# Gathered groups of a graph layer: plain row fetches, sums by quarters and a one-hot placement

## The chip, the cores and the metric

The kernel runs on one core of one Trainium2 chip. The metric is the device time of the launch in microseconds (us). The core has a matrix engine (TensorE, PE in the profile; its weight loads are PEld), a vector engine (VectorE, DVE), an activation engine (ScalarE, ACT), a general engine (GpSimd, POOL) and a queue engine that issues most transfers (SyncE, SP). Each works through its own list of instructions in order and waits for the others by semaphores.

## The reference

One layer of a graph network on 6250 nodes with 64 features and 206250 edges, sorted by the node they point to:

```
h   = relu(layernorm(x))
msg = h[src] + edge_feat
agg = segment_sum(msg, dst, 6250)
out = x + relu(agg @ W1 + b1) @ W2 + b2
```

W1 is 64 x 128 and W2 is 128 x 64. All is float32. `h[src]` is a lookup of one row per edge, and `segment_sum` adds the rows that share a destination. On average a node has 33 edges.

## The kernel before

The edges are padded to 202 **groups** of 1024 (`G`; eight per partition, `J = 8`). They are treated in two ways.

**Counted groups** (the first 178, `GA`). The nodes that they reach are cut into 22 **blocks** of 252 nodes (`NW = 22`). For a block, `count` makes a matrix that says how many edges go from each source node to each of the block's nodes. It takes 14 steps per block: in every second step DVE makes two one-hot tiles (`hot_lo` and `hot_key`, L702), in each step PE multiplies six pairs of them into PSUM (L712) and ACT copies the counts to bfloat16 (L714). One block later PE multiplies the counts with h, which is kept in three bfloat16 parts (`product`, L747 and L750). So h[src] is never fetched for these edges. Their edge features are summed apart, in chunks of 42 nodes: `load` brings a chunk (SP queue, L375), `chunk_hot` makes a one-hot of 21 columns on DVE (L384), `chunk_sum` multiplies one-hot and features in four column groups of PE, a quarter of the chunk's edges in each (L396), ACT copies the result (`by_node`, L399), and `chunk_place` puts the four quarters to their columns by a constant 0/1 matrix (`select`, L408) inside the block's PSUM.

**Gathered groups** (the last 24, `GP = 24`) reach the rest of the nodes. `load_h` brings a group's edge features (SP queue, L824, one transfer of 256 KB) into a tile `pfeat` of four buffers. `fetch_h` then issues eight indirect transfers on the POOL queue (`gather`, L256), each of which fetches one row of h per partition from a table in device memory and **adds** it to `pfeat` on the way. The groups go in pairs. `sum_groups` makes a one-hot of 42 columns for each of the two (`hotp`, L425), multiplies the summed rows with it (16 matmuls, features as the weights, two column groups, L429), ACT copies the result (`sum_p`, L432), and `add_sums` adds it to the node sums `agg` at a column that is read into a register (L418).

After that, each block goes through the two dense layers (`mlp_hidden` L799, `mlp_product` L806, `mlp_add` L813, `mlp_store` L817).

**Order of the work.** The order of instructions is written out by hand (`manual_schedule`). A loop over 310 steps calls `count` for each, and a table `before`, a list `later` and some counters put all else between the steps. Where a pair of gathered groups goes is planned: `queue` holds what POOL has still to issue, each with a planned cost (`GATHER_US = 2.12` for a row gather, `WORDS_US = 2.6` for two gathers of edge words), `clock(n)` is the planned time of step n (1.7 us per step in the first block, 1.35 us behind it), and a pair is put behind step n when the planned end of its gathers, and 4 us (`LAND_US`), lie before `clock(n)`. What has not found a place by the last step follows behind the loop. The planner only sets the order; on the chip, engines wait for what has not come yet.

**The opening** (until about 41 us) finds where each block's edges lie: gathers of `rows` and `words` on POOL, searches on ACT (`seek`, L272), the packing of source and destination into one word per edge (`dstn`, two operations of DVE, L515, which need the source numbers that PE has turned and ACT copied to `srcl`, L505), a write of the packed list (L518, issued from ACT's list), and the layer norm. L510 copies to `row2` the first node of each gathered group, spread by PE over the partitions (`pe`, L509).

The lines that the change touches, cut to the core:

```
parts_of[g] = work.tile([P, J, D], F32, name="pfeat", bufs=4)            # load_h
gather(parts_of[g][:, j, :], table, src_p[:, ...j:...j+1], OP.add)       # fetch_h
hot = work.tile([P, J, W], F32, tag="hot", name="hotp")                  # sum_groups, W = 42
nc.tensor.matmul(pa[k:k + D, b, :], tiles[b][:, j, :], hot[:, j, :], ...)  # k = 0 or 64
to = agg[:, ds(bases.pop(g + b), W)]                                     # add_sums
nc.vector.tensor_tensor(to, to, pa[:, b, :], op=OP.add)
```

Of the kernel before, what the change touches and what calls it, by code (L numbers as in the profile page):

```python
# [9 lines left out]
F32 = mybir.dt.float32  # L10
# [8 lines left out]
P = 128  # L19
N = 6250  # L20
E = 206250
D = 64
# [15 lines left out]
W = 42  # L38
# [10 lines left out]
WR = 128  # L49
WR_BITS = 7  # L50
# [4 lines left out]
GP = 24  # L55
# [16 lines left out]
NW = 22  # L72
# [26 lines left out]
GATHER_US = 2.12  # L99
WORDS_US = 2.6  # L100
# [8 lines left out]
def gnn_kernel(ctx: ExitStack, tc: tile.TileContext, x, src_t, dst_t, dst_g, edge, w1, b1, w2, b2, out):  # L109
# [34 lines left out]

    firstp_i = small.tile([1, GP], I32, name="firstp_i")
    nc.scalar.dma_start(firstp_i.rearrange("o (q h k) -> o q h k", h=2, k=1),
                        dst_g[GA // 2:G // 2, :, 0:1].unsqueeze(0))
# [44 lines left out]
    edge_w = small.tile([P, 4], F32, name="edge_w")  # L192
    for k, of in enumerate((1.0 - W, 0.5, WQ - 0.5, SPAN - 0.5)):
        nc.gpsimd.memset(edge_w[:, k:k + 1], of)
# [16 lines left out]
    select = consts.tile([P, W], F32, name="select")  # L211
    nc.gpsimd.memset(select, 1.0)
    for q in range(JQ):
        part = select[q * QP:(q + 1) * QP, :]
        nc.gpsimd.affine_select(part, part, pattern=[[1, W]], compare_op=OP.is_equal, fill=0.0, base=-QS[q],
                                channel_multiplier=-1)
        nc.gpsimd.affine_select(part, part, pattern=[[0, W]], compare_op=OP.is_ge, fill=0.0, base=WQ - 1,
                                channel_multiplier=-1)
# [36 lines left out]
    def gather(rows, source, index, op=OP.bypass):  # L255
        nc.gpsimd.indirect_dma_start(out=rows, out_offset=None, in_=source,  # L256
                                     in_offset=bass.IndirectOffsetOnAxis(ap=index, axis=0), compute_op=op)
# [24 lines left out]
    dst_p = consts.tile([P, GP, J], I32, name="dst_p")  # L282
    rel_p = dst_p.bitcast(F32)
# [74 lines left out]
    bank = ps.tile([P, GB * D], F32, name="bank", bufs=1)  # L358
# [54 lines left out]
    def add_sums():  # L413
        for g, pa in to_add:
            for b in range(GB):
                done_at[g + b] = max(made)
                to = agg[:, ds(bases.pop(g + b), W)]
                nc.vector.tensor_tensor(to, to, pa[:, b, :], op=OP.add)  # L418
        to_add.clear()

    def sum_groups(g, tiles):
        pa = bank[:, :GB * W].rearrange("p (b w) -> p b w", b=GB)
        for b in range(GB):
            hot = work.tile([P, J, W], F32, tag="hot", name="hotp")
            nc.vector.tensor_tensor(hot, rel_p[:, g - GA + b, :].unsqueeze(2).to_broadcast([P, J, W]),  # L425
                                    iota[:, :W].unsqueeze(1).to_broadcast([P, J, W]), op=OP.is_equal)
            for j in range(J):
                k = j % 2 * D
                nc.tensor.matmul(pa[k:k + D, b, :], tiles[b][:, j, :], hot[:, j, :],  # L429
                                 start=(j < 2), stop=(j >= J - 2))  # L430
        sum_p = work.tile([P, GB, W], F32, name="sum_p", bufs=1)
        nc.scalar.activation(sum_p, pa, AF.Copy)  # L432
        to_add.append((g, sum_p))
# [72 lines left out]
    firstp = small.tile([1, GP], F32, name="firstp")  # L506
    nc.vector.tensor_copy(firstp, firstp_i)
    pe = ps.tile([P, GP], F32, tag="po", name="pe", bufs=1)
    nc.tensor.matmul(pe, ones[0:1, :], firstp, start=True, stop=True)  # L509
    nc.scalar.activation(row2[:, GA:], pe, AF.Copy)  # L510
# [20 lines left out]
    pools[0].__exit__(None, None, None)  # L531
    counts.append(ctx.enter_context(pools[1]).tile([P, HI, BN + NX * V], BF16, name="counts1"))
# [13 lines left out]
    src_p = consts.tile([P, GP * J], I32, name="src_p")  # L546
    nc.sync.dma_start(src_p, src_t[:, GA * J:])
    nc.sync.dma_start(dst_p, dst_t.rearrange("p (g j) -> p g j", j=J)[:, GA:, :])

    def table_rows(index, tmp):  # L550

        nc.vector.tensor_scalar(tmp, index, LO_BITS, None, op0=OP.logical_shift_right)
        nc.vector.tensor_scalar(index, index, P - 1, None, op0=OP.bitwise_and)
        nc.vector.scalar_tensor_tensor(index, index, float(HI), tmp, op0=OP.mult, op1=OP.add)

    def find_groups():

        nc.vector.tensor_scalar(base_i[:, GA:], row2[0:1, GA:], 0.0, float(N - 1), op0=OP.max, op1=OP.min)
        nc.vector.tensor_tensor(rel_p, dst_p, row2[:, GA:].unsqueeze(2).to_broadcast([P, GP, J]), op=OP.subtract)
# [96 lines left out]
    bad = small.tile([P, 9], F32, name="bad")  # L656
    found = small.tile([1, 5], F32, name="found")

    def outside(k):
        over = late.tile([P, NWIN + NX], BF16, tag="part", name="over")[:, :GP * J]  # L660
        nc.scalar.activation(over, rel_p.rearrange("p g j -> p (g j)"), AF.Relu, scale=1.0 if k else -1.0,
                             bias=edge_w[:, 0:1] if k else 0.0, accum_out=bad[:, k:k + 1])

    def inside(n):
        which, k = divmod(n, 2)
        a = (keys[:, 1, :, 0], rel[:, :NC].rearrange("p c q k -> p (c q k)"))[which]
        over = late.tile([P, NWIN + NX], BF16, tag="part", name="over")[:, :a.shape[1]]
        nc.scalar.activation(over, a, AF.Sign, scale=-1.0 if k else 1.0,  # L668
                             bias=edge_w[:, (1, 3 - which)[k]:(2, 4 - which)[k]], accum_out=bad[:, n + 2:n + 3])

    def limits():
        nc.vector.tensor_reduce(bad[:, 6:9], bad[:, :6].rearrange("p (n k) -> p n k", k=2), AX.X, OP.add)
        nc.vector.tensor_tensor(needed, row2[0:1, GA:], needed, op=OP.is_lt)
        nc.vector.tensor_reduce(found[:, 3:4], needed, AX.X, OP.max)
        pb = ps.tile([P, 3], F32, tag="po", name="pb", bufs=1)
        nc.tensor.matmul(pb, ones, bad[:, 6:9], start=True, stop=True)
        known["b"] = pb
# [3 lines left out]
    def limits_found():  # L681
        pb = known.pop("b")
        nc.vector.tensor_scalar(found[:, 0:1], pb[:1, 0:1], 0.0, None, op0=OP.is_gt)
        nc.vector.tensor_scalar(found[:, 1:3], pb[:1, 1:3], 2.0 * EA, None, op0=OP.not_equal)
        nc.vector.tensor_reduce(found[:, 4:5], found[:, :4], AX.X, OP.add)
        nc.vector.tensor_copy(odd_i, found[:, 4:5])
# [133 lines left out]
    parts_of = {}  # L820

    def load_h(g):
        parts_of[g] = work.tile([P, J, D], F32, name="pfeat", bufs=4)
        nc.sync.dma_start(parts_of[g].rearrange("p j d -> p (j d)"),  # L824
                          edge[g * P * J:(g + 1) * P * J, :].rearrange("(p j) d -> p (j d)", j=J))
# [5 lines left out]
    def fetch_h(g):  # L831
        if g not in parts_of:
            load_h(g)
        for j in range(J):
            queue.append((GATHER_US, lambda j=j: gather(
                parts_of[g][:, j, :], table[:, :], src_p[:, (g - GA) * J + j:(g - GA) * J + j + 1], OP.add)))
        queue.append((0.0, lambda: fetched.setdefault(g, pool[0])))
# [9 lines left out]
    def features_h(g):  # L847
        read_bases(g, GB)
        sum_groups(g, [parts_of.pop(g + b) for b in range(GB)])
        for b in range(GB):  # L850
            if g + 4 + b < G:
                fetch_h(g + 4 + b)
# [10 lines left out]
    table_rows(src_p, src_hi)  # L863
# [9 lines left out]
    fetch_pair(2)  # L873
    for k in range(3):
        norm_h(k)
    load(1)
    for g in range(GA + 2, GA + 4):
        load_h(g)
    todo = {}

    def then(k, f):
# [3 lines left out]
        1: [lambda: seek(12, 3), lambda: chunk_nodes(0)],  # L885
# [3 lines left out]
        5: [lambda: place(12, 3)],  # L889
        7: [lambda: norm_b(0)],  # L890
        9: [lambda: norm_b(1)],
        11: [lambda: norm_b(2)],
        13: [find_groups],
# [12 lines left out]
        112: [lambda: outside(1)],  # L906
        116: [lambda: inside(0)],
# [77 lines left out]
    for n, (b, s) in enumerate(steps):  # L985
# [23 lines left out]
        if n >= 3:  # L1009
            if h_next < G and fetched.get(h_next + 1, 1e9) + LAND_US <= clock(n):  # L1010
                features_h(h_next)
                h_next += GB
                add_later(n + 5)
            if n == 3:
                pool[0] = clock(n - 1) + OPENING_US
            pool_until(clock(n) + LAND_US)
# [31 lines left out]
    while h_next < G:  # L1048
        features_h(h_next)
        h_next += GB  # L1050
# [14 lines left out]
    odd = nc.values_load(odd_i, min_val=0, max_val=4)  # L1065
    with tc.If(odd > 0):
# [20 lines left out]
        with tc.For_i(0, G, 1) as g:  # L1087
            feat = work.tile([P, J, D], F32, tag="pfeat", bufs=4, name="feat2")
            hsrc = work.tile([P, J, D], F32, tag="pfeat", bufs=4, name="hsrc")
# [16 lines left out]
            with tc.For_i(0, more, 1) as w:  # L1106
                hot = work.tile([P, J, WR], F32, tag="hotr", bufs=1, name="hotr")
# [51 lines left out]
```

## Time and profile before

| what | value |
| --- | --- |
| time, three runs | 511.65, 514.52 and 520.31 us, median 514.52 us |
| the profiled execution | 511.06 us, of which 509.4 us between its first and last instruction (the span) |
| granted TensorE clock | 0.991 |
| busy share of the span | PE 87%, PEld 75%, DVE 82%, ACT 71%, POOL 81% |
| instructions | 19099 |
| bytes moved | 79.04 MB in 113544 packets, 155 GB/s |

The profile is one execution. Busy times are a sum over each engine, so the same span holds all of them beside each other. "Issue" is time in which an engine waited for nothing that the profile shows. A group of instructions is told by line, engine, operation and tiles, with its count, its busy time and the mean of one. The chain of work is followed back from the last instruction, each step to what released it.

### The profile page before, as it was taken

The page shows a single profiled execution, that of the slowest core. Times are in us where ns is not written, and L with a number is a line of the kernel's source. Part 1 is how long each engine was busy: PE and PEld are TensorE (multiplying, and loading weights), DVE is VectorE, ACT ScalarE, POOL GpSimd, SP SyncE. Part 2 cuts the span into 40 slices and gives each one's busy share as a digit, 9 for nine tenths or more (in the row PEclk, how much of TensorE's full clock was granted, in tenths as well). Part 3 has the DMA queues.
Part 4 walks back from the last instruction along what each step waited for, and adds up shares of the span by engine and source line. Part 5 has one row for each costly group of instructions (what it writes and reads, how often), then busy time and mean ns, then how long its engine had stood idle before and what let it go on. Part 6 is the DMA issues. An engine that isn't in the chain of part 4 may idle for free.

```text
span 509.4 us, 19099 instructions
## 1 busy us (share of the span) xinstructions
PE 442.5 (87%) x8183; PEld 380.9 (75%) x8184; DVE 416.8 (82%) x632; ACT 359.1 (71%) x530; POOL 412.0 (81%) x265
## 2 busy tenths in 40 slices
PE   1226678889999988989989999999999999999893
PEld 1115557778888877778878888888888988888782
DVE  4789999698999969979879879799698798698521
ACT  6648867678777656997757777767777777667611
POOL 6676888888874888889888888888888888898880
PEclk9999899999999999999999999999999999999997
DMA  8848722566686566565665676586675766846560
GB/s 235 250 127 276 204 31 59 118 166 165 170 219 188 141 153 161 140 144 163 146 173 108 145 191 145 147 191 147 152 188 144 194 148 140 200 105 153 118 146 17
DMA packets 113544, 79.04 MB, mean 155 GB/s; under 512 B 32920, under 2 KB 108686, under 8 KB 113230
## 3 DMA queue, kind: packets, MB, share of 16 engines
q1 hardware_dynamic: 83962, 65.99, 43.5%
q0 software_dynamic: 29200, 10.25, 17.0%
q10 hardware_dynamic: 292, 1.52, 1.0%
q8 instruction: 66, 1.08, 0.9%
q14 instruction: 24, 0.20, 0.1%
HBM read 73.74 MB, written 3.99 MB: 153 GB/s over the span
## 4 chain that ended last, share of the span: by engine, by line
PE 69%; DVE 17%; issue 4%; ACT 4%; DMA 3%; POOL 1%; DVEq 0%; ACTq 0%; POOLq 0%
PE pc L712 21%; PE pv L747 19%; PE pv L750 11%; PE bank L396 9%; DVE hot_key L702 6%; DVE hot_lo L702 5%; PE pv L408 3%; PE ph L799 2%; PE po L806 2%; PE bank L429 2%; ACT counts L714 2%; DMA rows<-in_dst_g,row_i 1%; DMA dstq<-in_dst_g,cols_i 1%; ACT over L668 1%; POOL rows L256 1%
## 5 line engine op out<-in xcount | busy, mean ns | idle before, releaser
L256 POOL DMA_INDIRECT pfeat<-table,src_p x192 | 361.4, 1882 | 61.3 <-issue 55.2
L714 ACT ACTIVATE counts<-pc 128x882 bf16<-128x882 f32 x310 | 276.8, 908 | 48.5 <-PE pc L712 33.9
L712 PE MATMUL pc<-hot_key,hot_lo 128*128 128x147 bf16 x1860 | 174.0, 231 | 25.8 <-DVE hot_key L702 13.8
L712 PEld LDWEIGHTS <-hot_lo 128*128 128x128 bf16 x1860 | 134.2, 99 | 49.3 <-DVE hot_key L702 18.1
L702 DVE TENSOR_TENSOR hot_lo<-iota_lo,keys 128x1536 bf16<-128x1536 bf16 x155 | 147.9, 954 | 26.6 <-PE pc L712 26.0
L702 DVE TENSOR_TENSOR hot_key<-iota_key,keys 128x1776 bf16<-128x1776 bf16 x155 | 167.0, 1078 | 0.0
L747 PE MATMUL pv<-counts,h 128*128 128x252 bf16 (+1 forms) x1078 | 147.8, 271 | 0.1
L747 PEld LDWEIGHTS <-h 128*128 128x128 bf16 x1078 | 98.7, 97 | 8.0 <-issue 0.2
L750 PE MATMUL pv<-counts,h 128*64 128x252 bf16 (+1 forms) x1078 | 75.4, 274 | 0.0
L399 ACT ACTIVATE by_node<-bank 128x128 f32<-128x128 f32 x66 | 18.4, 278 | 58.2 <-PE bank L396 58.2
L396 PE MATMUL bank<-feat,hot 128*21 128x64 f32 x3168 | 58.6, 223 | 0.7 <-DVE hot L384 0.7
L396 PEld LDWEIGHTS bank<-feat,hot 128*21 128x21 f32 x3168 | 47.2, 102 | 13.7 <-issue 10.7
L750 PEld LDWEIGHTS <-h 128*64 128x64 bf16 x1078 | 53.9, 111 | 3.3 <-issue 0.2
L384 DVE TENSOR_TENSOR hot<-rel,iota 128x504 f32<-128x504 bf16 x66 | 44.8, 679 | 6.4 <-PE bank L429 5.5
L425 DVE TENSOR_TENSOR hotp<-dst_p,iota 128x336 f32<-128x336 f32 x24 | 11.7, 504 | 17.4 <-PE bank L396 17.2
L256 POOL DMA_INDIRECT words<-packed,first_i x15 | 20.5, 1367 | 4.6 <-issue 3.7
L256 POOL DMA_INDIRECT rows<-in_dst_g,row_i x15 | 17.0, 1132 | 8.7 <-ACT inrow L272 3.0
L408 PE MATMUL pv<-select,by_node 128*64 128x42 f32 x264 | 21.1, 243 | 0.0
L408 PEld LDWEIGHTS pv<-select,by_node 128*64 128x64 f32 x264 | 13.2, 136 | 8.3 <-issue 0.6
L801 ACT ACTIVATE hid<-ph,b1s 128x252 f32<-128x252 f32 (+1 forms) x25 | 11.7, 466 | 8.4 <-PE ph L799 7.2
L759 DVE TENSOR_TENSOR sums<-sums,pv 128x252 f32<-128x252 f32 x22 | 9.0, 411 | 9.6 <-PE pv L750 9.6
L799 PE MATMUL ph<-sums,w1s 128*128 128x252 f32 (+1 forms) x50 | 15.4, 390 | 1.6 <-DVE sums L418 1.1
(172 smaller groups left out, 259.0 us busy)
## 6 DMA issues: line engine op xcount, KB each, us to landing
feat<-in_edge SPq DMA_DIRECT2D x132, 384.0 KB
pfeat<-in_edge SPq DMA_DIRECT2D x24, 256.0 KB
pfeat<-table,src_p POOLq DMA_INDIRECT x192
out_y<-y SPq DMA_DIRECT2D x24, 63.0 KB
xs<-in_x SPq DMA_DIRECT2D x4, 315.0 KB
dstn<-in_dst_g SPq DMA_DIRECT2D x1, 1024.0 KB
table<-xl SPq DMA_DIRECT2D x2, 512.0 KB
packed<-dstn ACTq DMA_DIRECT2D x1, 768.0 KB
```

Source lines behind the costliest of these rows:

```text
L256: nc.gpsimd.indirect_dma_start(out=rows, out_offset=None, in_=source, in_offset=bass.IndirectOffsetOnAxis(ap=index, axis=0), compute_op=op)
L384: nc.vector.tensor_tensor(hot_of[u][:, :n].rearrange("p c j w -> p (c j) w"), rel[:, c:c + n].rearrange("p c q k -> p (c q k)").unsqueeze( ...
L396: nc.tensor.matmul(bank[q * QP:q * QP + WQ, i * D:(i + 1) * D], hot[:, i, j, :], feat[i][:, j, :], start=(k == 0), stop=(k == JP - 1))
L399: nc.scalar.activation(by_node[u][:, :n].rearrange("p c d -> p (c d)"), bank[:, :n * D], AF.Copy)
L408: nc.tensor.matmul(pvs[b][0][i * D:(i + 1) * D, a:a + CN], of[:, i, :], select, start=False, stop=False)
L425: nc.vector.tensor_tensor(hot, rel_p[:, g - GA + b, :].unsqueeze(2).to_broadcast([P, J, W]), iota[:, :W].unsqueeze(1).to_broadcast([P, J, ...
L702: nc.vector.tensor_tensor(hot.rearrange("p t (m o) -> p t m o", o=2), iota_k.rearrange("p (m o) -> p m o", o=2).unsqueeze(1).to_broadcast( ...
L712: nc.tensor.matmul(pc[:, k, m * K:(m + 1) * K], hot_lo[:, j, :], hot_key[:, j, :K], start=True, stop=True)
L714: nc.scalar.activation(counts[b % 2][:, :, s * ST * V:(s + 1) * ST * V].rearrange("p h (k m) -> p h k m", k=2), pc[:, :, :ST // 2 * K].rea ...
L747: nc.tensor.matmul(pv, h3[:, h, :2 * D], of, start=(h == 0 and not clear), stop=False)
L750: nc.tensor.matmul(pv[k:k + D, :], h3[:, h, 2 * D:], of, start=False, stop=(h >= HI - 2))
L799: nc.tensor.matmul(ph[:, :n], w1s, agg[:, start[b]:start[b + 1]], start=True, stop=True)
```

## The change

Gathered groups grow from 24 to 32, and the blocks of counts shrink from 22 to 21. With them go 6 of the 132 chunks, one of 15 lists of words and one of 5 lists of chunk destinations.

`fetch_h` fetches rows of h **without the addition**, into a tile of its own (`hsrc`, four buffers). `pfeat` keeps two buffers and the edge features alone; it is loaded by four transfers of 64 KB per group, since a group's edges now lie by quarters: quarter q of the group (256 edges in order) sits in two of the eight columns of all partitions.

The sums go as in the chunks: the one-hot has 21 columns and is made once per pair, each of a group's 16 tiles (8 of `pfeat`, 8 of `hsrc`) is a matmul with the one-hot as weights in the column group of its quarter, ACT copies the four partial results (`by_group`). Two steps later `place_groups` makes a one-hot `sel` on DVE from the quarters' offsets (`off_p`) and PE places the quarters with it into 52 columns of the same PSUM bank. `add_sums` adds from that bank, 64 partitions per group.

```
-W = 42
+W = 52
-GP = 24
+GP = 32
+PQ = 4
+PK = J // PQ
-NW = 22
+NW = 21
-GATHER_US = 2.12
-WORDS_US = 2.6
+GATHER_US = 1.4
+WORDS_US = 2.7
...
+    def hot_groups(g):
+        hot = work.tile([P, GB, J, WQ], F32, tag="hot", name="hotp")
+        r = rel_p[:, g - GA:g - GA + GB].rearrange("p b q k -> p (b q k)")
+        nc.vector.tensor_tensor(hot..., r..., iota[:, :WQ]..., op=OP.is_equal)
+        return hot
+    def sum_groups(g, hot, tiles):
         for b in range(GB):
+            for i, of in enumerate(tiles[b]):
+                for k in range(PK):
+                    for q in range(PQ):
+                        j = q * PK + k
+                        nc.tensor.matmul(bank[q * QP:q * QP + WQ, b * D:(b + 1) * D], hot[:, b, j, :], of[:, j, :],
+                                         start=(i == 0 and k == 0), stop=(i == 1 and k == PK - 1))
+        by_node["h", g] = work.tile([P, GB, D], F32, tag="by_node", name="by_group")
+        nc.scalar.activation(by_node["h", g]..., bank[:, :GB * D], AF.Copy)
+    def place_groups(g):
+        of = by_node.pop(("h", g))
+        sel = work.tile([P, GB, W], F32, name="sel", bufs=1)
+        nc.vector.tensor_tensor(sel, iota_wr..., off_p[:, g - GA:g - GA + GB]..., op=OP.is_equal)
+        for b in range(GB):
+            nc.tensor.matmul(bank[b * D:(b + 1) * D, GB * D:], of[:, b, :], sel[:, b, :], start=True, stop=True)
+        to_add.append(g)
...
+    for q in range(PQ):
+        nc.tensor.matmul(pe[q * QP:(q + 1) * QP, 1, :], ones[0:1, :QP], firstp[:, :, q], start=True, stop=True)
+    nc.scalar.activation(row2[:, GA:], pe[:, 0, :], AF.Copy)
+    nc.vector.tensor_tensor(off_p, pe[:, 1, :], row2[:, GA:], op=OP.subtract)
...
+    def by_quarters():
+        for q in range(PQ):
+            for b in range(PQ):
+                nc.gpsimd.tensor_copy(src_p[b * QP:(b + 1) * QP, :, q, :], src_s[q * QP:(q + 1) * QP, :, b, :])
...
     def load_h(g):
+        if g < G:
+            parts_of[g] = work.tile([P, J, D], F32, name="pfeat", bufs=2)
+            for b in range(PQ):
+                nc.sync.dma_start(parts_of[g][b * QP:(b + 1) * QP]..., rows[b])
     def fetch_h(g):
+            rows_h[g] = work.tile([P, J, D], F32, name="hsrc", bufs=4)
+                queue.append((GATHER_US, lambda j=j: gather(rows_h[g][:, j, :], table, src_p[...])))
...
+                at(n + 2, place_groups, h_next)
```

The instruction `off_p` stands on DVE's list ahead of the two `dstn` operations. The 16 copies of `by_quarters`, which put the source numbers into the new layout, stand on POOL's list between the second pair of word gathers and the first gather of h. `find_groups` now takes the destinations by quarters and is followed by two PE transposes and one ACT copy (`turn_groups`). The counts' second tile is opened at step 10, since it takes the memory of the lists. With the planner's new costs the 16 pairs stand behind steps 28, 48, 69, 88, 104, 122, 139, 155, 172, 188, 205, 221, 238, 255, 271 and 288 of 296; before, the 12 pairs stood behind steps 39, 70, 101, 128, 153, 178, 203, 228, 253, 278 and 303 of 310, and the last behind the loop.

## The prediction

> **What bounds the kernel now.** I first read the chain that ended last, by engine, and the groups of instructions.
>
> ```profile
> PE 69%; DVE 17%; issue 4%; ACT 4%; DMA 3%; POOL 1%; DVEq 0%; ACTq 0%; POOLq 0%
> ...
> L256 POOL DMA_INDIRECT pfeat<-table,src_p x192 | 361.4, 1882 | 61.3 <-issue 55.2
> ...
> L396 PE MATMUL bank<-feat,hot 128*21 128x64 f32 x3168 | 58.6, 223 | 0.7 <-DVE hot L384 0.7
> ```
>
> The chain runs through PE. But POOL's 192 gathers are busy for 361.4 us with 55.2 us of "issue" between them, and POOL waits for almost nothing else. One gather costs 1.88 + 0.30 = 2.18 us, and from its first at 44.84 us POOL never pauses for long. So two lines end side by side, which the timeline shows:
>
> ```profile
> 494.27 2.86 PE L750 MATMUL pv<-counts,h 128*64 128x252 bf16 x49
> 495.25 1.55 POOL L256 DMA_INDIRECT pfeat<-table,src_p  x1 [0.30 <-issue]
> ...
> 498.37 1.14 PE L429 MATMUL bank<-hotp,pfeat 128*64 128x42 f32 x32
> ```
>
> PE's last product ends at 497.13, POOL's last gather at 496.80; the last pair follows 1.57 us behind that gather, and 11 us of tail behind it. What a block costs PE stands in the chain in order of time; the same place of successive blocks is marked by the 13 narrow products:
>
> ```profile
> 310.36 0.87 PE pv L750 x13
> ...
> 329.20 0.87 PE pv L750 x13
> ...
> 332.94 1.06 PE bank L429 x32
> ...
> 349.20 0.87 PE pv L750 x13
> ```
>
> A block without a pair takes 18.84 us, one with a pair 20.00. PE is busy for all of 310 to 329.
>
> **PE's line, part by part** (from the profiled span, 509.4).
> - One block less: -18.84.
> - Pairs. Before, 11 in the loop at 1.14 (32 matmul instructions each): -12.5. After, 16 pairs of 64 instructions (each float32 matmul is two), one-hot as weights, in four column groups. L396 is this form: its 48 instructions take 0.80 in the chain, 0.0167 each, so 1.07; the placement is 4 instructions like L408's four, 0.32. 16 x 1.39 = +22.2.
> - The last pair leaves the tail. Its matmuls held the dense layers of the last block by 0.5 us, and the last part's hidden layer waited 1.14 us for its sums (L418): -1.3 in all, as the single buffer of the dense layers' PSUM keeps some of it.
> - One list of chunk destinations (three transposes, 0.9) and half a pair of words (0.4) less: -1.3.
> - Opening. `off_p` waits on DVE for ACT's copy L510, ahead of `dstn`:
>
> ```profile
> 15.08 1.22 DVE L515 SCALAR_TENSOR_TENSOR dstn<-dstn,srcl 96x1024 int32<-96x1024 int32 x1 [5.16 <-ACT srcl L505]
> ...
> 16.72 0.22 ACT L510 ACTIVATE row<-pe 128x24 f32<-128x24 f32 x1
> 16.95 1.22 DVE L515 SCALAR_TENSOR_TENSOR dstn<-dstn,srcl 96x1024 int32<-96x1024 int32 x1 [0.64 <-ACT row L510]
> ...
> 18.60 0.51 ACT L272 ACTIVATE inrow<-rows,nhalf 128x256 bf16<-128x256 int32 x1 [1.66 <-DVE dstn L515]
> ```
>
> The first `dstn` now starts behind 16.94, and `off_p` (0.16) and the two `begins` operations (0.5), which ran at 9.4, stand before it. Both `dstn` end at 20.05 instead of 18.17. Queued behind are the packed list's write on ACT's list, then `inrow`, and for that wait POOL's next `rows` gathers and the norm: +1.9. `table_rows` on 256 columns instead of 192: +0.3.
> - The copies on POOL may hold DVE in block 0, where DVE sets the pace: 0 to 16 x 0.2; I take +1.3.
> - The second `hotp` of a pair waited for the chunk sum's buffer (17.2 us of DVE over 7 waits), and PE then waited for the hot tiles (0.96 and 1.43 us at 476 and 447). One `hotp` per pair removes that: 0 to -3, I take -1.5.
>
> Sum: 509.4 - 18.84 - 12.5 + 22.2 - 1.3 - 1.3 + 1.9 + 0.3 + 1.3 - 1.5 = 499.7, and with the 1.66 us around the span 501.3.
>
> **Taken at nothing.** DVE per pair: 2 x 0.50 + 2 x 0.21 before; one 0.50, a `sel` and two sums of about 0.2 after; DVE is 85% busy behind PE (16.4 of 19.2 us in the block above). ACT's `by_group` is `sum_p`'s size. SP issues 128 transfers of 64 KB instead of 24, some 0.36 us each, ahead of the next `feat` loads, but waits 274 us for buffers; and `pfeat` has a pair's time, 24 us, to land. If that cover fails, PE waits some us per pair.
>
> **POOL's line.** The trace has no plain gather of h. Its bounds are the plain rows of the opening (0.945) and the adding ones (1.88). Its delay is seen in the rows:
>
> ```profile
> 104.61 0.99 POOL L256 DMA_INDIRECT words<-packed,first_i  x1 [0.30 <-issue]
> 105.65 0.95 DVE L702 TENSOR_TENSOR hot_lo<-iota_lo,keys 128x1536 bf16<-128x1536 bf16 x1
> 105.91 1.53 POOL L256 DMA_INDIRECT words<-packed,first_i  x1 [0.30 <-issue]
> ...
> 264.23 1.08 DVE L702 TENSOR_TENSOR hot_key<-iota_key,keys 128x1776 bf16<-128x1776 bf16 x1
> 264.56 2.17 POOL L256 DMA_INDIRECT pfeat<-table,src_p  x1 [0.30 <-issue]
> ```
>
> A gather that begins while a hot operation runs is held to its end: the adding one then takes 1.42 us more, the plain one 0.8. Of the 186 adding gathers from 60 us on, 44 began with no DVE operation under way and took 0.02 us over the unhindered 1.55; 131 began under a hot operation and took 0.46 more. So a plain one saves 0.6 us of its own time and none of the delay. Two ways give its cycle: the 14 plain gathers from 68 us on average 1.234, with the gap 1.53; a gather of 0.945 laid through the DVE rows of 80 to 480 us gives 1.495, and the two long waits of before (5.33 and 7.00 us, 8.6 over the mean, on 192) add 0.045: 1.54. I take 1.534; 256 make 392.7 us, against 418 for 192 before. Bounds: 1.49 to 1.58.
>
> Start: POOL was free at 41.81, now 44.0, and makes 16 copies of 32 x 64 numbers. Small POOL operations of the opening take 0.21 to 0.27, no row shows one beside the hot operations. Floor 0.3 each, ceiling one hot operation (1.0) each; nearest are the gathers between 45 and 76, held 0.26 on average, so 0.55: 8.8 us, first gather at 52.8. The table's rows land at about 47, so this hides no more than 3 of it. Fourteen other gathers at 1.59: 22.3.
>
> [...]
>
> End: the last pair stands behind step 288, with 7 steps to go. Before, from the pair behind step 303 (474.05) to the end were 35.35 with 6 to go. One step more (+1.35), the tail (-1.3), the placement (+0.35): 35.75. So 52.8 + 392.7 + 22.3 + 1.57 + 35.75 = 505.1, and with 1.66: **506.8**. That is later than PE's 501.3. The places of the pairs confirm it: they come every 16.5 steps, some 23.7 us of PE, while POOL needs 24.5 for 16 gathers; PE, in order, waits at the later pairs with all counts queued behind it.
>
> **Forecast: 507 us**, 0.8% under the profiled 511.06. The median of the runs, 514.52, is 0.7% above that execution; 2% is about what a measurement of this kernel can tell from no change, and the comparison is to be made against the profiled one: faster means under 500.8, slower over 521.3.
>
> **Rivals.**
> - *PE's line ends last* (0.34): 501, from 498 to 504. For it: between 80 and 230 us the laid gathers need only 1.44 to 1.47, and DVE slows POOL less whenever PE waits. Against: 1.55 between 300 and 440. About half of it is faster by 2%.
> - *Starved gathers*, on the slower side (0.17): POOL waits through a row of DVE operations, as at 227.92 (5.33) and 450.88 (7.00). A shorter cycle asks more often. At one long wait in 55 gathers instead of 96 the cycle is 1.61: 527. It decides from 1.59.
> - *The copies wait for one DVE operation each* (0.09): first gather at 60, the end at 514.
> - *The plain gather is no cheaper* (0.02): 2.18 each, some 672. Against it stand all `words` rows.
>
> The forecast keeps 0.36 (own range 503 to 518, with a tenth of it below 500.8 through shorter copies and cycle together); 0.02 is left for mishaps. Faster: 0.17 + 0.04 = 0.21. Slower: 0.17 + 0.02 + 0.01 = 0.20. Same: 0.59. The range 498 to 522 leaves out the starved case, the dear gather and the end of PE's.
>
> **What would show it.** A mean of the `hsrc` gathers near 1.23; first gather near 53; `dstn` ending near 20; pair sums of some 1.1 us; PE waiting for `hsrc` transfers at the last pairs; POOL's last gather some 37 us before the end. The forecast is wrong if PE never waits for a gather (501), or if the mean passes 1.3.

## The result, and the profile after

The changed kernel takes 531.85 us (median of four runs, 529.18 to 536.62) against 513.09 us before: a ratio of 1.039 with an interval of 1.029 to 1.050, so slower, 25 us from the forecast and outside the range. The profiled execution is 529.18 us with a span of 527.4.

First the parts of the page after: the busy engines, the chain that ended last by engine, and the gathers' group (busy, mean ns of one, idle ahead and its releaser).

```profile
PE 444.4 (84%) x8545; PEld 375.9 (71%) x8546; DVE 403.6 (77%) x627; ACT 346.7 (66%) x516; POOL 380.3 (72%) x347
...
PE 63%; DVE 12%; POOL 5%; issue 4%; ACT 4%; DMA 3%; DVEq 0%; ACTq 0%; POOLq 0%
...
L262 POOL DMA_INDIRECT hsrc<-table,src_p x256 | 325.2, 1270 | 78.0 <-issue 70.4
```

The term on which the forecast rested came out near its price: a plain gather costs 1.27 us. But POOL is not what ends last. Its last gather, in the timeline, ends 51 us ahead of the span's end, where before it was 13 us:

```profile
474.80 1.56 POOL L262 DMA_INDIRECT hsrc<-table,src_p  x1 [0.30 <-issue]
```

The list of waits (engine, line, what it waited for: us in total, times, longest) says who is late instead:

```profile
DVE sums L425 <- ACT by_node L405: 40.8, 11, 6.7
...
PE pc L760 <- DVE hot_key L750: 27.1, 14, 4.7
```

Before, DVE's additions of the group sums (then L418) waited some 2.8 us in the whole run, and PE waited 13.8 us for `hot_key`. The group on the page before, and the line in its list of waits:

```profile
L418 DVE TENSOR_TENSOR sums<-sums,sum_p 128x42 f32 x24 | 5.0, 208 | 2.8 <-PE ph L799 1.5 <-ACT counts L714 0.7
...
PE pc L712 <- DVE hot_key L702: 13.8, 12, 4.7
```

Now DVE stands for 40.8 us ahead of the additions of eleven of the sixteen pairs, and PE waits twice as long for the hot tiles that DVE makes behind them. One such place in the timeline, DVE, ACT and PE together (start, duration, and in brackets the wait):

```profile
120.59 0.68 DVE L390 TENSOR_TENSOR hot<-rel,iota 128x504 f32<-128x504 bf16 x1
...
122.60 0.33 PE L453 MATMUL bank<-sel,by_group 128*64 128x52 f32 x4
...
126.64 0.87 PE L402 MATMUL bank<-feat,hot 128*21 128x64 f32 x48
127.66 0.28 ACT L405 ACTIVATE by_node<-bank 128x128 f32<-128x128 f32 x1 [0.28 <-PE bank L402]
127.97 0.43 DVE L425 TENSOR_TENSOR sums<-sums,bank 64x52 f32 x2 [6.70 <-ACT by_node L405]
128.43 0.96 DVE L750 TENSOR_TENSOR hot_lo<-iota_lo,keys 128x1536 bf16<-128x1536 bf16 x1
129.30 1.11 DVE L750 TENSOR_TENSOR hot_key<-iota_key,keys 128x1776 bf16<-128x1776 bf16 x1
...
130.47 0.57 PE L760 MATMUL pc<-hot_key,hot_lo 128*128 128x147 bf16 x6 [2.96 <-DVE hot_key L750]
```

The placed sums (L453) are finished at 122.9. The addition that reads them starts at 127.97, 0.03 us after ACT has copied a chunk's sums out of *other columns of the same tile* `bank`. DVE does nothing for 6.70 us, `hot_lo` and `hot_key` of the next pair of steps stand behind the addition in its order, and PE, which had a lead of DVE's tiles to live on, uses it up and stands for 2.96 us. The places of PE's steps confirm it: step 49 starts 4 us later than before, step 112 16, step 182 23, and step 294, the last but one of now 296, 39 (each by its first matmul at L760, then L712); the kernel before had 15 more behind it.

Behind 75 us PE has five waits of more than 2.5 us, and a second loss follows three of them: over the next 6 us the mean granted clock is 0.72 there, and 1.00 behind the other two. Stretches of 2 us, with PE's busy time first and the granted clock third from the end:

```profile
128.00:130.00 2.00, 0.00 (x0) 0.00 (x0) 1.96 (x4) 0.00 (x0) 1.65 (x2) 1.00 0.55 160
130.00:132.00 2.00, 1.53 (x17) 1.34 (x17) 2.00 (x3) 0.91 (x1) 1.70 (x2) 0.91 0.92 283
132.00:134.00 2.00, 2.00 (x21) 1.44 (x20) 2.00 (x3) 0.91 (x1) 1.66 (x2) 0.50 0.07 16
134.00:136.00 2.00, 2.00 (x22) 1.94 (x20) 1.42 (x3) 1.32 (x2) 1.42 (x2) 0.74 0.09 16
136.00:138.00 2.00, 2.00 (x29) 1.68 (x26) 1.97 (x5) 1.98 (x3) 1.70 (x2) 1.00 0.29 70
```

PE stands for 3 us and is then granted half its clock for some 3 us more.

### The profile page after: what moved, and what is told of

Same layout as the page of the kernel before. It is cut to its first block, busy times and chain, and to the rows that moved or that the text cites. A ratio compares the mean times of both kernels' runs of the same rounds, so it can differ in the third digit from the quotient of the medians.

```text
span 527.4 us, 19970 instructions
## 1 busy us (share of the span) xinstructions
PE 444.4 (84%) x8545; PEld 375.9 (71%) x8546; DVE 403.6 (77%) x627; ACT 346.7 (66%) x516; POOL 380.3 (72%) x347
## 3 DMA queue, kind: packets, MB, share of 16 engines
q0 software_dynamic: 9600, 11.96, 11.3%
## 4 chain that ended last, share of the span: by engine, by line
PE 63%; DVE 12%; POOL 5%; issue 4%; ACT 4%; DMA 3%; DVEq 0%; ACTq 0%; POOLq 0%
PE pc L760 18%; PE pv L795 16%; PE pv L798 9%; PE bank L402 8%; DVE hot_key L750 5%; DVE hot_lo L750 4%; PE bank L442 3%; POOL hsrc L262 3%; PE pv L414 2%; PE ph L847 2%; PE po L854 2%; DMA hsrc<-table,src_p 2%; ACT counts L762 2%; POOL src_p L582 1%; POOL words L262 1%
## 5 line engine op out<-in xcount | busy, mean ns | idle before, releaser
L262 POOL DMA_INDIRECT hsrc<-table,src_p x256 | 325.2, 1270 | 78.0 <-issue 70.4
L762 ACT ACTIVATE counts<-pc 128x882 bf16<-128x882 f32 x296 | 265.4, 908 | 69.9 <-PE pc L760 58.3
L760 PE MATMUL pc<-hot_key,hot_lo 128*128 128x147 bf16 x1776 | 169.8, 233 | 40.8 <-DVE hot_key L750 27.1
L760 PEld LDWEIGHTS <-hot_lo 128*128 128x128 bf16 x1776 | 129.0, 100 | 65.8 <-DVE hot_key L750 32.2
L750 DVE TENSOR_TENSOR hot_lo<-iota_lo,keys 128x1536 bf16<-128x1536 bf16 x148 | 141.4, 955 | 34.2 <-PE pc L760 33.3
L750 DVE TENSOR_TENSOR hot_key<-iota_key,keys 128x1776 bf16<-128x1776 bf16 x148 | 159.6, 1078 | 0.0
L795 PE MATMUL pv<-counts,h 128*128 128x252 bf16 (+1 forms) x1029 | 142.1, 272 | 0.0
L795 PEld LDWEIGHTS <-h 128*128 128x128 bf16 x1029 | 94.7, 98 | 7.9 <-issue 0.2
L425 DVE TENSOR_TENSOR sums<-sums,bank 64x52 f32 x32 | 6.6, 206 | 46.5 <-ACT by_node L405 40.8
L445 ACT ACTIVATE by_group<-bank 128x128 f32<-128x128 f32 x16 | 4.5, 281 | 20.7 <-PE bank L442 13.9
L807 DVE TENSOR_TENSOR sums<-sums,pv 128x252 f32<-128x252 f32 x21 | 8.7, 415 | 10.4 <-PE pv L798 10.0
```

Source lines behind the costliest of these rows:

```text
L750: nc.vector.tensor_tensor(hot.rearrange("p t (m o) -> p t m o", o=2), iota_k.rearrange("p (m o) -> p m o", o=2).unsqueeze(1).to_broadcast( ...
L760: nc.tensor.matmul(pc[:, k, m * K:(m + 1) * K], hot_lo[:, j, :], hot_key[:, j, :K], start=True, stop=True)
L762: nc.scalar.activation(counts[b % 2][:, :, s * ST * V:(s + 1) * ST * V].rearrange("p h (k m) -> p h k m", k=2), pc[:, :, :ST // 2 * K].rea ...
L795: nc.tensor.matmul(pv, h3[:, h, :2 * D], of, start=(h == 0 and not clear), stop=False)
```

## The experiments

The theory after this reading (A): the additions wait for the chunk sums' copy because both read the same tile `bank` in PSUM (the memory into which PE writes its sums); DVE loses its lead, PE starves and slows. Its rival (B): POOL's queue, as forecast, sets the pace, and DVE's idle time only shows it. Ratios are to the kernel before on the same chip; runs 1 to 4, 5 to 8 and 9 to 11 shared one each, so across these groups a difference is safer read from the ratios.

| run | median, us | ratio (interval) | span | PE busy |
|---|---|---|---|---|
| changed kernel | 531.85 | 1.039 (1.029 to 1.050) | 527.4 | 444.4 |
| 1 sums copied to SBUF | 523.75 | 1.024 (1.019 to 1.028) | 522.6 | 443.3 |
| 2 and added two steps later | 522.78 | 1.022 (1.019 to 1.025) | 519.7 | 445.7 |
| 3 changed, half the gathers | 527.28 | 1.028 (1.024 to 1.033) | 526.3 | 444.8 |
| 4 before, sums read in PSUM | 520.61 | 1.018 (1.013 to 1.022) | 519.3 | 446.2 |
| 5 as 2, half the gathers | 498.15 | 0.968 (0.963 to 0.973) | 496.5 | 434.7 |
| 6 as 2, own tile for offsets | 526.03 | 1.022 (1.016 to 1.028) | 524.0 | 446.2 |
| 7 as 6, planner told 1.5 us | 512.05 | 0.994 (0.991 to 0.998) | 511.2 | 440.7 |
| 8 as 7, list turned on PE | 505.02 | 0.981 (0.974 to 0.988) | 502.4 | 438.2 |
| 9 as 8, sums in PSUM again | 513.17 | 0.998 (0.995 to 1.000) | 511.4 | 440.1 |
| 10 as 8, planner at 1.4 again | 517.78 | 1.006 (1.004 to 1.008) | 517.3 | 444.0 |
| 11 as 8, planner told 1.57 us | 501.88 | 0.974 (0.973 to 0.976) | 500.2 | 436.7 |

### Runs 1 and 2: the additions read a copy in SBUF

```diff
+        placed = work.tile([P, W], F32, name="placed", bufs=1)
+        nc.scalar.activation(placed, bank[:, GB * D:], AF.Copy)
-        to_add.append(g)
+        to_add.append((g, placed))
...
-                nc.vector.tensor_tensor(to, to, bank[half, GB * D:], op=OP.add)
+                nc.vector.tensor_tensor(to, to, placed[half, :], op=OP.add)
```

Run 2 also has `add_later(n + 7)` for `add_later(n + 5)`.

> The changed kernel with one edit: ACT copies the placed sums of a pair (128 x 52) from PSUM to SBUF right behind the placement, and the additions to the node sums read the copy instead of the PSUM bank. Theory A (VectorE's additions wait for the bank, which the chunk sums also use; VectorE so loses its lead and PE then waits for the hot tiles): the 40.8 us that VectorE waits ahead of the additions fall below 15, PE's waits for the hot tiles (22.4 us behind 75 us) fall below 12, and the time falls by 12 to 20 us, from 531 to 511 to 519; POOL's line, whose last gather ends at 476, then allows no less than 513. Theory B (POOL's gathers set the pace, as predicted): the waits move to the gathers and the time stays within 4 us of 531.

> The copy of the run before, and the additions stand seven steps behind the pair instead of five, so that they are five behind the placement. Theory A: what is left of VectorE's wait goes too, below 5 us; the time is 508 to 515. Theory B: within 4 us of 531. If the distance does nothing, the time is within 3 us of the kernel with the copy alone.

The wait for `by_node` is gone from both lists (in run 1 the additions wait 4.8 us for the new copy itself); the additions' groups of the changed kernel and of run 2:

```profile
L425 DVE TENSOR_TENSOR sums<-sums,bank 64x52 f32 x32 | 6.6, 206 | 46.5 <-ACT by_node L405 40.8
```

```profile
L425 DVE TENSOR_TENSOR sums<-sums,placed 64x52 f32 x32 | 6.8, 213 | 5.5 <-ACT counts L764 3.2 <-PE ph L849 2.0
```

But the time fell by 8 and 9 us only, half of what was expected. 41 us of DVE's waiting had become nothing, and PE's waits behind 75 us fell only from 34.2 to 24.7 us; the two steps more changed nothing that can be told. The waits of run 2 show what had come up from below:

```profile
DVE dstq L347 <- DMA dstq<-in_dst_g,cols_i: 5.7, 2, 5.5
...
PE bank L442 <- DMA hsrc<-table,src_p: 8.3, 5, 3.3
```

PE waits for gathered rows (2.0 us in the changed kernel), and DVE for a gather of chunk destinations that POOL issues late behind the rows of `h`.

### Run 3: half of the gathers, in the changed kernel

```diff
-                    rows_h[g][:, j, :], table[:, :], src_p[...])))
+                    rows_h[g][:, j, :], table[:, :], src_p[...])
+                    if j < J // 2 else None))
...
-    hot[:, b, j, :], of[:, j, :],
+    hot[:, b, j, :], of[:, j % (J // 2) if i else j, :],
```

> The changed kernel with half of the gathers of h left out: four of a group's eight rows per partition are fetched, and the matmuls of the other four read these again, so PE's work and the whole order are the same and part of the sums is left out of the result. POOL has 128 gathers instead of 256. Theory A: no gain beyond the two waits of PE for gathers (2 to 4 us), 526 to 532. Theory B: POOL's line ends 200 us earlier and the time falls to what PE needs, at most 515.

POOL's busy time fell from 380 to 217 us and the kernel's time by 4.6 us, with intervals that overlap; DVE's wait for `by_node` stayed at 38.4 us:

```profile
DVE sums L425 <- ACT by_node L405: 38.4, 10, 5.9
```

In the changed kernel the gathers are not the limit: A, not B.

### Run 4: the same wait put into the kernel before

The kernel before copies its placed sums to SBUF (`sum_p`) and adds that copy. Here they get columns of their own in the bank and DVE reads them there.

```diff
-    bank = ps.tile([P, GB * D], F32, name="bank", bufs=1)
+    bank = ps.tile([P, GB * D + GB * W], F32, name="bank", bufs=1)
...
-        pa = bank[:, :GB * W].rearrange("p (b w) -> p b w", b=GB)
+        pa = bank[:, GB * D:].rearrange("p (b w) -> p b w", b=GB)
...
-        sum_p = work.tile([P, GB, W], F32, name="sum_p", bufs=1)
-        nc.scalar.activation(sum_p, pa, AF.Copy)
-        to_add.append((g, sum_p))
+        to_add.append((g, pa))
```

> The kernel before with one edit: the pair's sums get columns of their own in the PSUM bank, ACT's copy of them is left out, and the additions read the bank. All else, gathers and counts too, is as before. Theory A: VectorE now waits ahead of the additions, some 2 to 3 us at each of 11 pairs where about 3 us were waited in all, PE waits 1 to 1.5 us more per pair for hot tiles, and the time grows by 8 to 16 us over the kernel before. Theory B, or a cause elsewhere in the change: within 3 us of the kernel before.

8.5 us slower, with nothing of the change but this edit, and the same line in its list of waits:

```profile
DVE sums L418 <- ACT by_node L399: 14.1, 7, 3.0
```

ACT has a copy less to make, and the kernel loses (by the interval, 1.3 to 2.2%). That shows the wait and what it costs on a kernel in which nothing else differs. Why the one read waits for the other is a question of its own, and stands with the step that failed below.

### Run 5: both at once

Run 2 with half of the gathers, as in run 3.

> The kernel with the copied sums and the later additions (519.7 us span), and half of the gathers of h left out: the sums of a group read each of its four fetched columns twice, so its output is not the layer's. In the kernel with the copy, PE still waits 8.3 us for gathered rows and DVE 5.5 us for the dstq gather, which POOL issues late at 162 us. Theory C (with the additions' wait gone, POOL's queue is the second limit): both waits go, and the time falls by 8 to 14 us to 508 to 514. Theory D (what is left over the kernel before is PE's own: 16 pairs of more work and a lower clock): within 3 us of 522.8. Half of the gathers did nothing for the changed kernel itself (527.3 against 531.9), where the additions' wait stood first.

498.15 us, 10 below the range of theory C. Taken alone, the one edit gave 9.1 us and the other 4.6; together they give 33.7 (by the ratios 9, 6 and 36). Each of the two limits hid the other, and either alone looked like a small matter. Between runs 3 and 5, which differ only in how the additions read and when, lie 29.1 us (31 by the ratios): that is the additions' wait where nothing else stands in front. Between runs 2 and 5 lie 24.6 (28 by the ratios): that is POOL's lateness. It is not that fewer gathers hold up DVE less: its hot operations take 0.956 and 1.077 us on average in run 2 and 0.954 and 1.075 in run 5.

Both show as waits and as clock. Runs 2 and 5 issue the same 8545 matmuls; behind 75 us PE waits 24.7 and 12.0 us (summed over its instructions), and its busy times differ by 11.0 us: together 23.7, against 23.2 of span. The mean granted clocks, 0.968 and 0.986, make some 9.7 us of the 11.0 (an estimate: 0.032 of 519.7 us less 0.014 of 496.5). So nearly half of what the waits cost here is PE's slower work behind them.

### Run 6: a tile of its own for the groups' offsets

In the opening `find_groups` writes the offsets over the source list, which POOL is still copying, and DVE waits 2.4 us.

```diff
-        rel_s = src_s.bitcast(F32).rearrange("p g b k -> p (g b k)")[:GP * PQ]
+        rel_s = pr.tile([GP * PQ, PK * P], F32, name="rel_s")
```

> The kernel with the copied sums and the later additions, and a tile of its own for the groups' offsets, which so far are written over the source list that POOL is still copying by quarters. The opening then has no DVE wait of 2.4 us for the 16 POOL copies. Theory E (that wait stands on PE's line, and the PE wait of 2.9 us behind it lowers the clock at 54 to 60 us): 3 to 5 us less, 518 to 520. Theory F (DVE makes it good later in block 0, or POOL's line ends last whatever DVE does): within 1.5 us of 522.8.

Theory F, and more: the ratio is the same, and POOL's part became worse. Its copies in the timeline of run 2, and of run 6:

```profile
46.52 3.91 POOL L584 COPY src_p<-src_s 32x64 int32<-32x64 int32 x12 [1.53 <-issue]
50.70 1.08 POOL L262 DMA_INDIRECT hsrc<-table,src_p  x1 [0.27 <-POOL src_p L584]
```

```profile
46.03 9.57 POOL L584 COPY src_p<-src_s 32x64 int32<-32x64 int32 x12 [1.16 <-issue]
55.87 1.39 POOL L262 DMA_INDIRECT hsrc<-table,src_p  x1 [0.27 <-POOL src_p L584]
```

Where DVE stands for 2.4 us of the time, twelve copies take 3.9 us; where it runs its hot operations instead they take 9.6, and the first gather comes 5.2 us later. DVE's wait had paid for itself.

### Runs 7, 10 and 11: what the planner counts for a gather

The order of PE's work is written down by a planner that places a pair where it believes its rows have landed. It counted 1.4 us for a gather and 1.35 for a step, a ratio of 1.04. A gather's cycle is 1.27 + 0.30 = 1.57 in the trace, and run 5's steps, where little waits, take 1.45 with the pairs among them (steps 60 to 294): 1.08. So PE's order asks for rows ahead of POOL throughout. Run 7 (from run 6) and run 11 (from run 8) change one number, and run 10 changes it back:

```diff
-GATHER_US = 1.4
+GATHER_US = 1.5
```

> As the run before it, and the planner counts 1.5 instead of 1.4 us for a gather, against its 1.35 us for a step: the traces show 1.56 us a gather, and a step of 1.40 where PE doesn't wait, so a ratio of 1.11 where the planner has 1.04. Pairs then are put later into PE's order, and the dstq and words gathers find a shorter queue. Theory C (POOL runs late against the plan, and PE's in-order queue turns it into waits): PE's waits for gathered rows fall from 8.3 to under 2 us and DVE's for dstq from 5.5 to under 1, and the time falls to 507 to 514. Theory D: within 3 us of the run before it.

> The best version so far with the planner's price of a gather back at 1.4 us. If the price by itself decides whether PE's order runs ahead of POOL (theory C): PE waits 5 to 10 us for gathered rows and the time is 511 to 518. If the earlier first gather alone was what mattered: within 2 us of 505.

> The best version so far with the price at 1.57 us, the measured cycle of a gather. The pairs stand later still in PE's order. If waits for gathered rows are left to be saved (2 us of them in the trace): 502 to 505. If the last pair is now pushed into the tail, behind which the dense layers stand: 506 to 511.

Run 7 is 14.0 us faster than run 6, as theory C said, though the waits fell less than it said: PE still waits 5.6 us for rows (under 2 was expected), all of it between 84 and 91 us, since POOL's first gather comes as late as 57.5, and DVE 2.9 us for `dstq` (under 1). Run 10 loses 12.8 us against run 8. Of the 14.9 us between their spans, 8.8 are PE's waits behind 75 us and 5.8 its longer busy time; its wait for rows rises from 2.0 to 11.3 us:

```profile
PE bank L442 <- DMA hsrc<-table,src_p: 11.3, 7, 3.1
```

Run 11 has no such line. Two pairs stand in its tail, where PE waits 2.0 and 1.3 us, and yet its median is 3.1 us below run 8's (the intervals of the two ratios touch). Runs 7 and 10 go the way of theory C, by the sizes given.

### Run 8: the list brought into quarters on PE

Two transposes and two ACT copies in the opening instead of POOL's 16 copies; the list comes in by four transfers instead of one, and DVE unpacks it in the new layout (both left out below). Run 8 also has 1.5 for a gather, and the offsets take the list's tile again.

```diff
-                nc.gpsimd.tensor_copy(src_p[b * QP:(b + 1) * QP, :, q, :], src_s[q * QP:(q + 1) * QP, :, b, :])
...
+        pt = ps.tile([P, PK, GP * PQ], F32, tag="po", name="psp", bufs=1)
+        for k in range(PK):
+            nc.tensor.transpose(pt[:, k, :], src_f.rearrange("r (k p) -> r k p", k=PK)[:, k], ident[:GP * PQ, :GP * PQ])
+        for k in range(PK):
+            nc.scalar.activation(src_p[:, :, :, k], pt[:, k].rearrange("p (q g) -> p g q", q=PQ), AF.Copy)
```

> As the run before it, and the source list is brought into quarters by two TensorE transposes and two ACT copies in the opening instead of 16 copies on POOL; the offsets may then take the list's tile again. The first gather of h can start at 44 to 46 us instead of 50.8 (POOL's two words gathers end at 42, the table lands at some 43). If POOL's queue is the limit, the time falls by another 4 to 6 us, to 503 to 509, below the kernel before (512.2); if PE's own work is, it stays within 2 us of the run before it.

The first gather starts at 45.1 us, and the time is 505.02 us, 7 less than run 7 and below the kernel before.

### Run 9: the additions' wait put back

Run 8 with the edits of runs 1 and 2 undone.

> The best version so far (sums copied to SBUF, later additions, planner told, list turned: 505.0 us, ratio 0.981) with the first of its parts undone: the additions read the placed sums in PSUM again, five steps behind the pair, as in the changed kernel. Theory A (they wait for the next chunk sum's copy out of the same PSUM bank, DVE loses its lead, PE starves and its clock falls): between the two kernels with half of the gathers this was worth 29 us; here POOL's queue hides a part, so 12 to 25 us more, 517 to 530. If the copy to SBUF had only moved the pairs against each other: within 4 us of 505.

8.2 us slower than run 8: less than the 12 to 25 expected, but beyond the 4 us of the other case. DVE waits for `by_node` seven times here, not eleven:

```profile
DVE sums L425 <- ACT by_node L405: 24.5, 7, 6.0
```

The pairs stand at other places, so fewer additions may have a chunk sum just ahead of them; that, and what POOL hides here, were not told apart.

**What combines best** is run 11: the change, with its placed sums copied to SBUF, its list turned on PE, and a planner that knows the gather's price. It takes 501.88 us, 2.6% less than the kernel before (2.4 to 2.7%).

## Why the prediction was wrong, step by step

- **The step that failed** is "Taken at nothing. DVE per pair": it counted the additions' durations (0.2 us each; 0.21 measured) and not what they read. Before, they read `sum_p` in SBUF; the change reads `bank` in PSUM, which the chunk sums use between step n + 2 and step n + 5. Its sentence "If that cover fails, PE waits some us per pair" speaks of the loads of `pfeat`; for DVE it gave a share of 85% and no wait, and none of its rivals has one. The slower outcomes that it allowed for (0.20) were starved or dear gathers, and neither is what came. DVE's waits are 46.5 us ahead of the additions; what they cost is 8 us in run 4, 8 in run 9, and 29 between runs 3 and 5.
  Why a *read* waits for another engine's read of other columns is not shown by the runs. No data passes between the two, and with the sums in SBUF the wait is gone (40.8 us for `by_node` in the changed kernel, none in run 2). Nor does the trace tell ACT's copy from PE's chunk sums ahead of it, which write the same tile until 127.51 in the place shown (126.64 + 0.87) and for which the copy itself waits; of the 6.70 us the copy accounts for the last 0.46. What was measured is that the addition starts 0.03 us after ACT's copy ends. A sum in a tile of its own was not tried, so whether the wait belongs to the memory or to the program's one tile `bank` is not shown.
- **PE's line** (501.3) came out close, though it was not what the kernel reached. Run 5, where neither limit stands, takes 498.15 (496.8 by its ratio). The pair's sum was priced at 1.07 us and took 1.05; the placement at 0.32 and took 0.27 to 0.33:

```profile
152.78 1.05 PE bank L442 x64
```

```profile
264.53 0.27 PE L453 MATMUL bank<-sel,by_group 128*64 128x52 f32 x4
```

  The 3 to 5 us that run 5 lies below it aren't traced to single terms.
- **POOL's line**, the forecast (506.8), did not end last. Of its terms: the gather 1.234 was 1.270 (cycle 1.57 for 1.534, 10 us over 256); the first at 50.8 instead of 52.8; the last at 476 instead of 468. What stands behind the last gather was taken as 37.3 us of fixed work (1.57 to the pair and 35.75 from there), but it is 51 us in the changed kernel, 40 in run 2, and 20 in runs 8 and 11: it depends on where the planner puts the last pairs and how late PE is by then. Its mechanism, "PE, in order, waits at the later pairs", is real (runs 2 and 10; in the changed kernel PE waits 2.0 us for rows, at one pair), and the sum left out its second half, the waits' effect on the clock.
- **Starved gathers** (cycle 1.59 and more) did not come to pass in the changed kernel: 1.57, with two gathers of over 4 us (4.36 at 245.23 and 4.34 at 249.89). In that kernel DVE stands still for 46.5 us ahead of the additions. In runs 8 and 11, where it hardly does (6.9 and 10.4 us), a gather takes 1.316 and 1.306, some 1.6 with the gap, and the time falls all the same. The rival's own 1.61 counts the long waits twice: 4.3 us over 55 gathers, on the laid 1.495, give 1.57.
- **The copies wait for one DVE operation each** is near where DVE runs (9.57 us for twelve in run 6, 0.8 each where an operation of 1.0 each was the ceiling; first gather at 55.9, not 60), and the changed kernel escaped it because DVE itself stood still (2.44 us; the same twelve copies take 4.43 us).
- **The opening**: `off_p` ahead of `dstn` was priced at 1.9 us. DVE waits 6.61 us for ACT there, as forecast, but ACT was earlier, and both `dstn` end at 18.98 against 18.17: 0.8. The first `hot_lo` starts 0.3 us later than before. The 1.3 us for copies that hold DVE were an estimate that no run shows: beside them, from 42.74 us on, its hot operations take 0.99 and 1.11, then 0.95 and 1.08 us, against 0.955 and 1.078 on average. Missed was DVE's 2.4 us behind POOL's copies.
- **The one-hot's wait for the chunk sums' buffer** (1.5 us gained) went as said: the changed kernel has no such line among its waits. Beside the 46.5 us of waits in the same place of DVE's order it is nothing.

## What to carry to other kernels

When an operand moves from SBUF to PSUM, its price can lie not in its duration (0.21 us an addition here) but in who else uses that tile (46.5 us of waits here), when the instruction's engine has the bound engine's next input queued behind it in its order; a copy on an engine with time to spare can be the cheaper way (ACT's `sum_p` takes 0.24 us, and run 4 lost 8.5 us without it). A planner's price list belongs to the change: when a transfer becomes cheaper or dearer, its ratio to a step must be measured anew (with 1.4 us for a gather instead of 1.5, run 10 lost 12.8 us against run 8). And two limits can hide each other: when taking one away gives less than its wait, take both away once before you call it small (9.1 and 4.6 us alone, 33.7 together).

## What was not expected of the hardware

The granted clock reacts to single waits in the middle of dense work. In the traces of the changed kernel and of runs 1 to 4, 6, 7, 9 and 10, PE waited 26 times for more than 2.5 us behind 75 us; in the 6 us after such a wait the mean granted clock was 0.50 to 0.75 in 22 cases and 1.00 in four (the changed kernel's at 320.93 and 422.80 are two of them). Behind waits of 1.0 to 1.55 us inside the loop that had no second one within a few us it was 1.00 each time, in every trace of the case (1.51 us at 116.66 in run 2, with 0.53 more right behind it, was followed by 0.72); between 1.6 and 2.1 us it went both ways. At 0.72 over 6 us, such a wait costs PE some 1.7 us on top of its length (an estimate: 0.28 of the 6 us). Single waits of 1.80 to 2.01 us were followed by 0.72 in four places (145.21 in run 10, 200.87 in run 4, 257.23 in run 8, 388.98 in run 6), and so was one of 1.64 with 0.37 behind it in the changed kernel (116.94); two of 1.91 and 1.88 in run 9 (159.61 and 214.99) were followed by 1.00. Why a wait of one length lowers the clock once and not another time is not shown. Stretches of run 2 behind its wait of 4.75 us, which ends at 167.46:

```profile
166.00:168.00 2.00, 0.54 (x5) 0.54 (x6) 2.00 (x4) 0.00 (x0) 1.70 (x2) 0.50 0.26 85
168.00:170.00 2.00, 2.00 (x14) 1.71 (x12) 2.00 (x4) 0.91 (x1) 1.39 (x3) 0.50 0.14 29
170.00:172.00 2.00, 2.00 (x21) 1.66 (x21) 1.97 (x4) 1.40 (x2) 1.70 (x2) 0.50 0.08 16
172.00:174.00 2.00, 2.00 (x63) 1.50 (x59) 1.45 (x2) 0.37 (x2) 1.69 (x2) 0.83 0.13 19
```

PE is busy all the time from 168 us on, and for 5 us of it at half its clock (third column from the end, as above).
